# One turn for the slice tokens' half-column products, and a switch time in the planner's model

## The chip, the cores and the metric

The kernel runs on one core of a Trainium2 chip. Its time is the device time of one execution in microseconds; the runs of one kernel are summed up by their median. A core has a matrix engine (PE, whose weight loads are listed as PEld), a vector engine (DVE), a scalar engine (ACT), a small general engine (POOL), and a queue that issues DMAs (SP).

## The reference

For each of 32 batches of x (512 tokens, 256 features, fp32), a graph network and a slice attention are added to x:

```python
# x = x + gnn(layernorm(x), adj);  x = x + ffn(layernorm(x))
out = relu(xn @ mlp1_w + mlp1_b)                 # 512 x 512
h   = out @ W_fc;  att = softmax(leaky_relu(f1[:, None] + f2[None, :]))
out = elu(elu(att @ h)) + out                    # residual
out = relu(out @ mlp2_w + mlp2_b)                # 512 x 256
h   = out @ W_hand; att = softmax(where(adj > 0, leaky_relu(...), -9e15))
x1  = x + relu(elu(elu(att @ h)) + out)
# ffn, 8 heads of 64, 64 slices
w   = softmax((xn2 @ W_x + b_x) @ W_slice / temp)        # per head
tok = (w.T @ (xn2 @ W_fx + b_fx)) / (w.sum(tokens) + 1e-5)
tok = softmax(tok W_q (tok W_k).T / 8) @ (tok W_v)
x   = x1 + (w @ tok) @ W_out + b_out
```

## The kernel before

One batch is one "age". The program is written batch by batch in 22 named steps: `load, norm1, mlp1, h, factors, p, pv, o1` in `front`, `mlp2, h2, e, p2, pv2` in `middle`, `norm2, w, sums, s1T, tokens, att, vo, gg, out` in `back`. No instruction is issued while it is written. A `Recorder` takes each one down with a cost from a model (`_cost`), finds which earlier ones it depends on, and `order` then works out one order for all of them, which `emit` issues. So every instruction has the same line, L255, in the profile, and groups are told apart by their tiles.

The order is made by list scheduling. Each engine takes, of the instructions that can start, the one with the smallest key. A first pass gives each instruction the key age x `PERIOD` + `TURNS[step]` (spread over the step by cost) and plans the first batches; the start times of batch 8 in that plan become the keys of every batch in the second pass, with `HEAD` and `TAIL` added for the first and last three. Instructions of up to four batches are mixed, so that PE finds work of one batch while another waits for DVE, ACT or a DMA. The PSUM tile `mm` has five buffers.

The names in the profile, in the order in which one batch meets them on PE:

- `mm<-xnT,w` (mlp1), `mm<-wfc,o0T` (h), `tr<-ident,ex` (factors), then `mm<-h,pT` (pv): 32 products in four quarters. Of each quarter DVE and ACT make u (`u<-mm,rd`, `m<-u`, two exponentials of m on ACT, `u<-m,u`) and DVE transposes blocks into `u_stage`. When all four are there, SP sends four scatters `scr<-u_stage` to DRAM and one load `o1T<-scr` back, which makes a full transpose; DVE adds o0T (`o1T<-o1T,o0T`).
- `mm<-o1T,w` (mlp2), `mm<-wh,o2T` (h2), then on DVE and ACT the masked logits e, which go through DRAM in the same way (`e_stage`, `p2T`), and `mm<-h,p2T` (pv2).
- x1 and the second layer norm (DVE's xn, `xn_stage`, a load into `xn_raw`), `mm<-weff,xn2T` (w), the softmax of w on DVE, `mm<-xn,w` (sums), and s1 through DRAM (`s_stage`, `s1T`).
- tokens: `mm<-s1T,wfx` are 16 products of 64 columns, each into one half of the partitions of a PSUM tile, and `mm<-nrow,bfx` two more into the halves. These 18 are the half-column products. Then `tok` (DVE), `mm<-tok,wqk`, `qbd`, `sm<-tok,qbd`, `mm<-wvo,tokbd`, `tr<-ident,attbd`, `attT`, `mm<-vo,attT`.
- `mm<-gg,wT` (out): 16 products, two DVE adds into x1 (`x<-mm,x`) and the store.

An fp32 product shows as two rows (two passes) on PE. In the first and the last batch the transposes are made on PE instead of through DRAM.

SP issues DMAs in its order and waits at each for what it needs. Seven loads a batch come back from DRAM scratch, and one buffer of scratch staging (`stage4`, `stage`) is shared by several of them.

Of the kernel before, what the change touches and what calls it, by code (L numbers as in the profile page):

```python
# [13 lines left out]
ENGINES = ("tensor", "vector", "scalar", "gpsimd", "sync")  # L14

TURNS = {
# [4 lines left out]
}  # L21
PERIOD, SPARE = 88.0, 0.00

HEAD, TAIL = (-3.1, -0.9, -0.1), (-1.0, -1.3, -1.0)


SAMPLE, SETUP = 8, 15.0
# [3 lines left out]
P = 128  # L31
# [4 lines left out]
class Recorder:  # L36
# [3 lines left out]
    SIGNAL = 0.06  # L40
    DRAIN = 0.17
    ISSUE, BEGIN, LAND, BEHIND = 0.45, 1.2, 0.9, 2.7
    KEPT = 1
    AHEAD = 3

    def __init__(self, nc):
        self.nc, self.ops, self.logs, self.age, self.step = nc, [], {}, -1, ""
        for engine in ENGINES:
            setattr(self, engine, _Recording(self, engine))

# [23 lines left out]
    def take(self, engine, method, args, kwargs):  # L74
        outs, ins = list(args[:1]), [x for x in args[1:] if isinstance(x, bass.AP)]
        for key, x in kwargs.items():
            if isinstance(x, bass.AP):
                (outs if key in ("out", "accum_out") else ins).append(x)
        op = _Op(engine, method, args, kwargs, self.age, self.step, len(self.ops))
        op.cost, op.lag = self._cost(op, outs[0], ins)  # L80
        before = {}
        for aps, writes in ((ins, False), (outs, True)):
            for ap in aps:
                if not hasattr(ap.tensor, "tag"):
                    continue
                lo, hi, bits = self._region(ap)
                log = self.logs.setdefault(ap.tensor.name, _Log(ap, self.age))
                if log not in op.logs:
                    op.logs.append(log)
                kept = []  # L90
                for entry in log.entries:
                    other, olo, ohi, obits, owrites = entry
                    if other is op:
                        kept.append(entry)
                        continue
                    if (writes or owrites) and olo < hi and lo < ohi and obits & bits:
                        before[other.index] = other
                    if not (writes and lo <= olo and ohi <= hi and not obits & ~bits):
                        kept.append(entry)
                kept.append((op, lo, hi, bits, writes))  # L100
                log.entries = kept
        for other in before.values():
            other.after.append(op)
        self.ops.append(op)

    def _cost(self, op, out, ins):


        def words(ap):
            return ap.size() // ap.ap[0][1]  # L110

        n = words(out)
        if op.method == "dma_start":
            side = next(ap for ap in (out, *ins) if ap.space != bass.MemoryType.DRAM)
            op.moving = out.size() * 4 / (215e3 if side.ap[0][1] <= P // 4 else 320e3)
            return self.ISSUE, 0.0
        if op.engine == "tensor":
            one = max(n / 1200 + 0.002, 0.109)
            if out.ap[0][1] == P // 2:
                one = max(n / 2400, 0.03)  # L120
            return (one if op.method == "transpose" else 2 * one), self.DRAIN
        if op.engine == "scalar":
            pointers = sum(isinstance(op.kwargs.get(k), bass.AP) for k in ("bias", "scale"))
            return 0.06 + n / 1200 + 0.09 * pointers + 0.19 * ("accum_out" in op.kwargs), 0.12
        if op.engine == "vector":
            n = max([n] + [words(x) for x in ins])
            single = op.method in ("tensor_copy", "tensor_scalar")
            fast = single and all(x.space != bass.MemoryType.PSUM for x in ins)
            pointers = sum(words(x) == 1 for x in ins) if n > 1 else 0
            return 0.07 + n / (1920 if fast else 960) + 0.065 * pointers, 0.1  # L130
        if n < 16:
            return (0.1 if op.method == "memset" else 0.3 if op.method == "tensor_scalar" else 1.1), 0.1
        return 0.2 + n / (480 if op.method == "tensor_tensor" else 960), 0.1

    def _schedule(self, ops, key, spare):
# [31 lines left out]
                    t = max(t, min(slots[log.tag]))  # L167
            return t

        done, moved = [], 0.0  # L170
        while len(done) < len(ops):
            best = None
            for e in ENGINES:
                can = [
                    (s, op)
                    for op in waiting[e]
                    if op.age <= oldest + self.AHEAD and (s := start_of(op)) is not None
                ]
                if not can:
                    continue  # L180
                t = max(free[e], min(s for s, _ in can))
                one = min((key(op), op.index, op) for s, op in can if s <= t)
                best = min(best or (t, *one), (t, *one))
            if best is None:
                raise RuntimeError("no operation can start")
            t, _, _, op = best
            waiting[op.engine].remove(op)
            for log in op.logs:
                if log not in until:
                    slots[log.tag].remove(min(slots[log.tag]))  # L190
                    turn[log.queue].pop(0)
                    until[log] = 0.0
            op.start, op.end = t, t + op.cost + op.lag
            free[op.engine] = t + op.cost
            if op.moving:
                moved = max(moved, t + self.BEGIN) + op.moving
                op.end = moved + self.LAND
                free[op.engine] = max(t + op.cost, moved - self.BEHIND)
            for log in op.logs:
                users[log] -= 1  # L200
                until[log] = max(until[log], op.end)
                if not users[log]:
                    slots[log.tag].append(until[log] + self.SIGNAL + spare)
            for later in op.after:
                if later not in left:
                    continue
                if later.engine != op.engine:
                    at = op.end + self.SIGNAL + spare
                else:
                    at = t + op.cost if op.engine == "tensor" else op.end  # L210
                later.ready = max(later.ready, at)
                left[later] -= 1
                if not left[later]:
                    waiting[later.engine].append(later)
            ages[op.age] -= 1
            while not ages.get(oldest, 1):
                oldest += 1
            done.append(op)
        return done

    def order(self):


        steps, keys, ends = {}, {}, {}
# [3 lines left out]
        for (age, step), ops in steps.items():  # L228
            at = TURNS.get(step, -1e5)
            till = TURNS[names[min(names.index(step) + 1, len(names) - 1)]] if age >= 0 else at  # L230
            costs = [op.cost if op.engine == "tensor" else 0.02 for op in ops]
            part = 0.0
            for op, cost in zip(ops, costs):
                keys[op] = age * PERIOD + at + part / sum(costs) * (till - at)
                part += cost
        for op in steps[-1, "setup"]:
            keys[op] = SETUP
        for op in self._schedule([op for op in self.ops if op.age < SAMPLE + 4], keys.get, SPARE):
            ends[op.age] = max(ends.get(op.age, 0.0), op.end)
        period = (ends[SAMPLE] - ends[SAMPLE - 4]) / 4  # L240
        starts = {step: [op.start for op in steps[SAMPLE, step]] for step in TURNS}
# [50 lines left out]
def adj_ffn_kernel(  # L292
# [39 lines left out]
    nc = Recorder(tc.nc)  # L332
# [11 lines left out]
    def mm_tile(shape):  # L344
        return psum.tile(shape, F32, tag="mm", name="mm", bufs=5)
# [52 lines left out]
    def load_x(b):  # L398
# [7 lines left out]
        out=ident, in_=ident, compare_op=OP.not_equal, fill=1.0, base=0,  # L406
# [157 lines left out]
    for p in range(NP):  # L564
        pv = mm_tile([P, D])
# [250 lines left out]
    def back(b, x1):  # L816
# [17 lines left out]
        w = new("w", [P, NT, INNER])  # L834
# [57 lines left out]
        s1T = med("s1T", (P, KD, INNER))  # L892
# [19 lines left out]

        nc.step = "tokens"

        pm = mm_tile([P, NP, G])
        for p in range(NP):
            for k in range(KD):
# [7 lines left out]
        for s in range(2):  # L925
            nc.tensor.matmul(
                pm[ts(s, C)], bfx[:, ts(s, C)], nrow[:, s], start=False, stop=True
            )

        def diagonal(dst, src):  # L930
            nc.vector.tensor_copy(dst(0), src(0))
# [128 lines left out]
```

## Time and profile before

| | us |
|---|---|
| runs (5): median, lowest to highest | 2727.99, 2725.32 to 2731.58 |
| the profiled execution's own time | 2726.07 |
| its span in the profile | 2724.3 |
| PE busy | 2669.1 (98%) |
| DVE busy | 2057.1 (76%) |
| ACT busy | 1118.5 (41%) |
| PE busy from 300 to 2536 us, a stretch of 2236 | 2221.82 |
| PE busy from 2536 us to the end, 188.3 | 167.15 |

A busy PE in these tables is one that has a product in its pipeline; it does not say that the products follow each other at full rate. So the text reads start times in the timeline, where the distance from one row's start to the next, divided by the passes in it, gives the pace. The columns of a timeline row are: start, length, engine, line, operation, out<-in, rows x columns of the array, output size, passes, and in brackets the engine's idle time before it with what ended it.

### The profile page before, as it was taken

Reading aid. Unit: us, or ns where it says so; the run is one execution under the profiler, and the core shown is the slowest. Engines: PE = TensorE matmul, PEld = TensorE weight load, DVE = VectorE, ACT = ScalarE, POOL = GpSimd, SP = SyncE. Lnnn points to the kernel's source line nnn. Section 1 sums busy time; section 2 is a strip of 40 time slices with the busy share of each in tenths; the row PEclk is TensorE's granted clock in tenths of the full one; section 3 lists DMA queues with packets and bytes.
Section 4 is the critical chain, followed back from the end, with each engine's and each line's share of the span. In section 5 each row is a group of like instructions: output and inputs, shape, how many; then the busy total and the mean of one; then the engine's idle time right before and its main releaser. Section 6 shows DMA issues by size and latency. Waiting matters only on the chain.

```text
span 2724.3 us, 34426 instructions
## 1 busy us (share of the span) xinstructions
PE 2669.1 (98%) x11965; PEld 1990.5 (73%) x11965; DVE 2057.1 (76%) x5126; ACT 1118.5 (41%) x2102; POOL 124.8 (5%) x233
## 2 busy tenths in 40 slices
PE   7999999999999999999999999999999999999997
PEld 5777777777777777777777777777777777777765
DVE  6577777887778877778877778777788777788775
ACT  2443344443444433444434444334444334444332
POOL 1000000000000000000000000000000000000000
PEclk9999999999999999999999999999999999999998
DMA  5226455655455555555455556555555555564521
GB/s 167 50 60 167 131 142 145 159 145 148 134 159 139 146 156 139 142 148 159 132 155 139 147 139 155 154 138 140 148 155 136 154 139 144 145 160 128 144 73 47
DMA packets 465077, 375.35 MB, mean 138 GB/s; under 512 B 86532, under 2 KB 382088, under 8 KB 464904
## 3 DMA queue, kind: packets, MB, share of 16 engines
q1 hardware_dynamic: 461568, 371.01, 51.3%
q10 hardware_dynamic: 3336, 2.14, 0.3%
q8 instruction: 95, 1.56, 0.2%
q14 instruction: 78, 0.64, 0.1%
HBM read 197.96 MB, written 175.11 MB: 137 GB/s over the span
## 4 chain that ended last, share of the span: by engine, by line
PE 75%; DMA 11%; DVE 8%; issue 2%; SPq 2%; ACT 2%; POOL 0%; ACTq 0%; DVEq 0%; POOLq 0%
PE mm L255 72%; DMA o1T<-scr 3%; DMA scr<-s_stage 3%; PE tr L255 2%; SPq L255 2%; DMA s1T<-scr 2%; DMA w_raw<-scr 2%; DVE u L255 1%; DVE u_stage L255 1%; PE sm L255 1%; DVE xn_stage L255 1%; DVE xn L255 1%; ACT m L255 1%; DVE w L255 1%; DVE vo L255 0%
## 5 line engine op out<-in xcount | busy, mean ns | idle before, releaser
L255 PE MATMUL mm<-wfc,o0T 128*128 128x257 f32 x2048 | 486.1, 379 | 0.0
L255 PEld LDWEIGHTS mm<-wfc,o0T 128*128 128x128 f32 x2048 | 386.2, 189 | 131.1 <-issue 84.9
L255 PE MATMUL mm<-h,pT 128*128 128x257 f32 (+1 forms) x2048 | 466.9, 382 | 0.4
L255 PEld LDWEIGHTS mm<-h,pT 128*128 128x128 f32 x2048 | 380.0, 189 | 62.5 <-ACT u L255 4.8
L255 DVE TENSOR_TENSOR x<-mm,x 128x512 f32<-128x512 f32 x64 | 44.2, 691 | 294.5 <-PE mm L255 294.5
L255 PE MATMUL mm<-xnT,w 128*128 128x512 f32 x512 | 250.3, 604 | 2.6 <-ACT xnT L255 2.2
L255 PE MATMUL mm<-weff,xn2T 128*128 128x512 f32 x512 | 251.3, 594 | 0.0
L255 PE MATMUL mm<-xn,w 128*128 128x257 f32 x1024 | 243.2, 380 | 6.3 <-DVE w L255 5.5
L255 PE MATMUL mm<-h,p2T 128*128 128x257 f32 x1024 | 242.0, 380 | 0.7 <-ACT p2T L255 0.7
L255 ACT COPY h<-mm 128x257 f32<-128x257 f32 (+1 forms) x384 | 142.6, 371 | 240.7 <-PE mm L255 235.9
L255 PE MATMUL mm<-gg,wT 128*128 128x256 f32 x1024 | 236.0, 379 | 0.0
L255 PE MATMUL mm<-o1T,w 128*128 128x512 f32 x512 | 227.7, 597 | 6.2 <-DVE o1T L255 5.7
L255 PEld LDWEIGHTS mm<-xn,w 128*128 128x128 f32 x1024 | 190.4, 189 | 37.6 <-ACT w L255 5.7
L255 PEld LDWEIGHTS mm<-gg,wT 128*128 128x128 f32 x1024 | 190.1, 190 | 35.0 <-issue 6.5
L255 PEld LDWEIGHTS mm<-h,p2T 128*128 128x128 f32 x1024 | 187.0, 190 | 28.2 <-ACT p2T L255 0.9
L255 PEld LDWEIGHTS mm<-o1T,w 128*128 128x128 f32 x512 | 95.0, 190 | 121.9 <-issue 91.3
L255 DVE STREAM_TRANSPOSE o_stage<-o2T 128x512 f32<-128x512 f32 x64 | 45.6, 712 | 172.1 <-ACT o2T L255 172.1
L255 ACT ACTIVATE e<-e,nmax 128x512 f32<-128x512 f32 x128 | 92.5, 722 | 199.5 <-DVE nmax L255 199.4
L255 ACT ACTIVATE m<-m 128x512 f32<-128x512 f32 x192 | 120.3, 626 | 131.2 <-DVE m L255 131.1
L255 PEld LDWEIGHTS mm<-xnT,w 128*128 128x128 f32 x512 | 93.2, 192 | 69.7 <-issue 51.5
L255 ACT ACTIVATE m<-m,neg 128x512 f32<-128x512 f32 x192 | 138.0, 719 | 3.6
L255 DVE SCALAR_TENSOR_TENSOR u<-m,u 128x512 f32<-128x512 f32 x192 | 131.6, 686 | 9.4 <-ACT m L255 7.8
(144 smaller groups left out, 3923.8 us busy)
## 6 DMA issues: line engine op xcount, KB each, us to landing
scr<-xn_stage SPq DMA_DIRECT2D x240, 128.0 KB, 2.6
scr<-u_stage SPq DMA_DIRECT2D x120, 256.0 KB, 4.1
o1T<-scr SPq DMA_DIRECT2D x30, 1024.0 KB, 5.8
scr<-e_stage SPq DMA_DIRECT2D x120, 256.0 KB, 4.6
p2T<-scr SPq DMA_DIRECT2D x30, 1024.0 KB, 5.3
scr<-w_stage SPq DMA_DIRECT2D x120, 256.0 KB, 4.4
w_raw<-scr SPq DMA_DIRECT2D x30, 1024.0 KB, 6.5
xt<-in_x_dram SPq DMA_DIRECT2D x32, 512.0 KB, 4.6
```

Source lines behind the costliest of these rows:

```text
L255: getattr(getattr(self.nc, op.engine), op.method)(*op.args, **op.kwargs)
```

## The change

Three things are changed. While the 18 half-column products are recorded, `joint` is set, and in the first pass they all get the same key, that of the step's start, so that the planner takes them one after the other. The model gets a time `SWITCH` of 0.14 that it adds wherever PE goes from a half-column product to a whole one or back, and its cost of a half-column pass goes up from at least 0.03 to at least 0.038. And the step times `TURNS`, `PERIOD`, `HEAD` and `TAIL` are others, and the first pass plans one batch more. No instruction is added or removed; only their order on the engines differs.

```diff
 TURNS = {
-    "load": -182.4, "norm1": -141.0, "mlp1": -121.9, "h": -81.6, "factors": -79.1, "p": -73.9,
-    "pv": -53.9, "o1": -53.9, "mlp2": -11.7, "h2": -4.8, "e": 4.9, "p2": 4.9, "pv2": 6.7,
-    "norm2": 28.2, "w": 93.5, "sums": 96.0, "s1T": 101.5, "tokens": 121.9, "att": 133.4,
-    "vo": 142.3, "gg": 151.6, "out": 181.5,
+    "load": 210.7, "norm1": 212.1, "mlp1": 213.6, "h": 289.8, "factors": 309.8, "p": 312.5,
+    "pv": 326.7, "o1": 327.2, "mlp2": 377.6, "h2": 386.3, "e": 387.3, "p2": 391.7,
+    "pv2": 406.4, "norm2": 422.6, "w": 489.3, "sums": 508.3, "s1T": 519.5, "tokens": 539.2,
+    "att": 569.4, "vo": 569.4, "gg": 595.3, "out": 606.3,
 }
-PERIOD, SPARE = 88.0, 0.00
-HEAD, TAIL = (-3.1, -0.9, -0.1), (-1.0, -1.3, -1.0)
+PERIOD, SPARE = 100.3, 0.00
+HEAD, TAIL = (-8.6, 2.8, 1.6), (-4.4, 7.3, 23.6)
...
+    SWITCH = 0.14
...
+        op.joint = self.joint
+        op.half = engine == "tensor" and outs[0].ap[0][1] == P // 2
...
-            if out.ap[0][1] == P // 2:
-                one = max(n / 2400, 0.03)
+            if op.half:
+                one = max(n / 2400, 0.038)
...
+            if op.engine == "tensor" and op.half != half:
+                t, half = t + self.SWITCH, op.half
             op.start, op.end = t, t + op.cost + op.lag
...
+            costs = [0.0 if op.joint else cost for op, cost in zip(ops, costs)]
...
-        for op in self._schedule([op for op in self.ops if op.age < SAMPLE + 4], keys.get, SPARE):
+        for op in self._schedule([op for op in self.ops if op.age < SAMPLE + 5], keys.get, SPARE):
...
         nc.step = "tokens"
+        nc.joint = True
         pm = mm_tile([P, NP, G])
...
+        nc.joint = False
```

In the order that comes out, PE goes to half-column products 35 times instead of 88 in the 32 batches.

More of the change, by code (lines that the diff above doesn't have):

```diff
@@ L47, in __init__ @@
         self.nc, self.ops, self.logs, self.age, self.step = nc, [], {}, -1, ""
+        self.joint = False
         for engine in ENGINES:
@@ L168, in start_of @@
             return t
-        done, moved = [], 0.0
+        done, moved, half = [], 0.0, False
         while len(done) < len(ops):
```

## The prediction

> **What bounds the kernel now.** I read the page's engine rows first, then PE's waits, then one middle period in PE's and SP's timelines.
>
> ```profile
> PE 2669.1 (98%) x11965; PEld 1990.5 (73%) x11965; DVE 2057.1 (76%) x5126; ACT 1118.5 (41%) x2102; POOL 124.8 (5%) x233
> PE mm L255 <- DMA s1T<-scr: 15.2, 15, 8.5
> PE mm L255 <- DVE o1T L255: 5.7, 10, 1.2
> ```
>
> PE bounds it, with few idle gaps; the two PE waits that come back are those for s1T and for o1T. "Busy" hides pace, so here are start times:
>
> ```profile
> 1590.04 9.25 PE L255 MATMUL mm<-h,pT 128*128 128x257 f32 x42
> 1599.47 0.30 PE L255 MATMUL mm<-s1T,wfx 128*64 128x64 f32 x2 [0.18 <-DMA s1T<-scr]
> 1599.70 3.60 PE L255 MATMUL mm<-h,pT 128*128 128x256 f32 x14
> 1603.24 0.69 PE L255 MATMUL mm<-s1T,wfx 128*64 128x64 f32 x16
> 1603.85 2.00 PE L255 MATMUL mm<-h,pT 128*128 128x256 f32 x8
> 1605.78 0.68 PE L255 MATMUL mm<-s1T,wfx 128*64 128x64 f32 x14
> 1606.39 0.65 PE L255 MATMUL mm<-nrow,bfx 4*64 4x256 f32 x4
> 1606.96 1.12 PE L255 MATMUL mm<-xnT,w 128*128 128x512 f32 x2
> ...
> 1619.20 5.77 PE L255 MATMUL mm<-gg,wT 128*128 128x256 f32 x26
> 1625.18 7.13 PE L255 MATMUL mm<-o1T,w 128*128 128x512 f32 x16 [0.21 <-DVE o1T L255]
> 1632.15 3.65 PE L255 MATMUL mm<-wh,o2T 128*128 128x258 f32 x16
> ...
> 1673.11 3.19 PE L255 MATMUL mm<-h,pT 128*128 128x257 f32 x14
> ```
>
> One period is 83.07: 35.14 from the first h,pT to o1T,w (half A), 47.93 from there to the next h,pT (half B). Over 27 periods the timeline gives 35.05 and 47.89. The half-column products come in three visits. Half A has a second chain, through DRAM:
>
> ```profile
> 1611.04 3.37 SPq L255 DMA_DIRECT2D scr<-u_stage  x4
> ...
> 1618.42 0.38 SPq L255 DMA_DIRECT2D o1T<-scr  x1
> ...
> 1624.44 2.50 DVE L255 TENSOR_TENSOR o1T<-o1T,o0T 128x512 f32<-128x512 f32 x4 [0.90 <-DMA o1T<-scr]
> ```
>
> The last u_stage ends at 1611.0, 20.9 after half A began; 7.4 later SP issues the load; it lands 6.0 later; the add takes 0.7; PE starts at once. In nearly all 27 periods o1T,w starts within 0.1 of that add: this chain, not PE, sets half A.
>
> **Part 1, one visit.** Three visits take 0.23 + 0.61 + 1.18 = 2.02 (row starts above). A single one is in the trace, in batch 2:
>
> ```profile
> 277.50 0.60 PE L255 MATMUL mm<-h,pT 128*128 128x256 f32 x2
> 278.02 1.15 PE L255 MATMUL mm<-s1T,wfx 128*64 128x64 f32 x32
> 279.11 0.65 PE L255 MATMUL mm<-nrow,bfx 4*64 4x256 f32 x4
> 279.68 0.70 PE L255 MATMUL mm<-xnT,w 128*128 128x512 f32 x1
> ```
>
> That is 1.66. Two h,pT passes before it take 0.52 where two at the pace of wh,o2T (16 passes in 3.49, the next row starts at 1635.64) take 0.43: 0.09 per entry. Saved per period: 0.36 + 2 x 0.09 = 0.54 of PE time. [...]
>
> The visit now stands behind the last h,pT, about 4.7 later than the first token product stood (11 h,pT products of 0.43). s1T landed 9.45 after the start of half A on average, and is now needed at 13.8: that wait (0.18 here, 0.33 on average) goes. Late next is xnT, landing at 15.3 (median) and needed at about 15.6.
>
> **Part 2, the retimed order.** All of this is read from the new order, its costs from rows. Before o1T,w PE loses 13 gg products (5.6) and two vo (0.86), and gains 12 wfc (5.2) and one transpose (0.1): half A has 1.17 less PE work, half B 1.17 more. PE alone would thus need 35.14 - 0.21 - 0.18 - 0.54 - 1.17 = 33.0 for half A, and 49.1 for half B.
>
> The u chain decides. DVE's queue before had, between tok and the last u_stage, the third quarter's u and u_stage, two xn, u and qbd (1607.08 to 1611.0). Now the third quarter stands before tok, and the fourth's u and u_stage right behind it. DVE's work from its fourth pT operation (ends 2.0 to 2.5 into half A) to tok was 12.9, with 1.9 idle; it becomes 12.9 + 1.85, so tok starts at 16.8. m of the last quarter ends at 16.0; ACT's exponentials (0.63, 0.72 and hops) give 17.5; u 0.6 and u_stage 0.7 make 18.8, against 20.9. With the same 7.4 + 6.0 + 0.7 (SP's order u, xn, o1T is unchanged, and the four xn_stage end at 21.9, before the u scatters are all issued at 22.2) o1T is there at 32.9, as PE arrives at 33.0. Bounds: no gain of the chain (35.05), and PE alone with the small waits in pv gone too (32.5).
>
> So half A goes from 35.05 to 33.0 and half B from 47.89 to 49.06: 82.1 against 82.94, 0.85 less, times 27 = **-23** (bounds +32 and -38).
>
> What else moves: x1's two adds go into the dense DVE stretch of e and w (+1.24, two bn_stats of 0.33 go out of it), while PE needs the last w 0.3 later there; before, w had 0.42 of slack, I keep about 0.15, price 0 to 0.5 a period. Behind these adds on SP now stand the store, the load of xt and p2T's load: the adds end 32.2 after o1T,w, so p2T issues at about 33.1 (33.5 before) and PE needs it at 41 instead of 40. xt lands at about 37.6, and DVE's bn_stats reach it at 38.0; a wait there would hold DVE, and with it f2m, ex and the pT chain queued behind on DVE, but PE needs ex 1.4 after it can be there. The store and gg are 20 later in a period, which nothing in the next batches waits for. tok, tokbd and qbd get longer cover (4 xnT products instead of 1), all at nothing.
>
> **Head.** In batch 2 PE's work from o1T,w to p2T is 27.0 in the new order, 34.1 in the old one. The rows give the chain's length there: o1T,w at 217.16, h,p2T at 256.15, 39.0, waits in between:
>
> ```profile
> 217.16 7.11 PE L255 MATMUL mm<-o1T,w 128*128 128x512 f32 x16
> ...
> 248.84 1.97 PE L255 MATMUL mm<-xn,w 128*128 128x257 f32 x8 [2.28 <-DVE w L255]
> 256.15 2.33 PE L255 MATMUL mm<-h,p2T 128*128 128x257 f32 x10
> ```
>
> DVE's order of e and w there is the same, so the chain stays and 7.1 more of it shows; 2 more where the factors' transposes stand 2.1 instead of 3.7 before h,pT: **+9** (3 to 13).
>
> **Tail.** The wait of 8.5 for s1T (longest of its row) gets 3 more of PE work ahead of it, and p2T's delay too; the last factors get less cover (about 6), e about 3, att about 3. Losses from the last three batches: 32 before, about 29 after: **-3** (-10 to +6).
>
> **Sum.** 2726.07 (span 2724.3) - 23 + 9 - 3 = 2709; the median of the runs lies 1.9 above the profiled one, so **2711**.
>
> **Rivals.** A (slower): u_stage doesn't come earlier, since DVE or ACT is late before tok. Then half A stays 35.05, while half B has its 1.17 more: 27 x 1.17 + 6 = +38, about 2765. It decides from a chain gain below 1.4 a period (1.17 + 6/27). For it: DVE is busy nearly without a gap from w to tok. Against: 1.9 idle in front of tok, and the order puts u_stage first. B (far faster): the chain comes in under PE, and the waits in pv vanish: 32.5 + 49.0 = 81.5, -38 + 6: 2696. C (no gain): the chain gains about 1.4, through a late nrow (slack 0.5) or w, and pays for itself with the head: 2722 to 2733. That the change doesn't join is excluded for the middle (18 in a row in 30 batches).
>
> **Chances.** Forecast 0.50, B 0.20, C 0.16, A 0.14. A measurement here can tell about 0.2% (5.5). Faster 0.73: forecast, B, and a little of C; same 0.12; slower 0.15: A and the rest of C. Range 2692 to 2732: B's end and C; it leaves out A and a little beyond B.
>
> **What would show it.** Right: one s1T row x32 per batch; no PE wait for s1T in the middle; u scatters 18.8 after the first h,pT, o1T,w at 33, periods near 82.1; a wait of about 12 before p2T in batch 2. Wrong: u scatters still at 20.9 with a longer wait of o1T,w (A); new PE waits for w, nrow, xnT or pT (C); more than 40 us of gain or loss in head and tail.

## The result, and the profile after

The changed kernel takes 2735.6 us (median of 35 runs), the kernel before 2727.5 (59 runs). The ratio is 1.0027, with a 95% interval from 1.0020 to 1.0034: **slower by 8 us**, where 2711 was forecast. The profiled executions have spans of 2736.6 and 2724.3.

PE's waits in the changed kernel, the first two rows (total, times, longest):

```profile
PE mm L262 <- DMA xnT<-scr: 16.2, 21, 1.6
PE mm L262 <- DVE o1T L262: 8.9, 10, 1.5
```

The row for s1T's transfer is gone, as forecast. In its place stands a wait for xnT, which the prediction held to be just in time, and the wait for o1T has grown. PE's timeline of one period shows where they sit:

```profile
1593.37 3.62 PE L262 MATMUL mm<-h,pT 128*128 128x257 f32 x16
...
1596.93 10.55 PE L262 MATMUL mm<-h,pT 128*128 128x257 f32 x48
1607.41 1.15 PE L262 MATMUL mm<-s1T,wfx 128*64 128x64 f32 x32
1608.50 0.65 PE L262 MATMUL mm<-nrow,bfx 4*64 4x256 f32 x4
1609.68 3.67 PE L262 MATMUL mm<-xnT,w 128*128 128x512 f32 x8 [0.54 <-DMA xnT<-scr]
...
1626.42 7.11 PE L262 MATMUL mm<-o1T,w 128*128 128x512 f32 x16
```

The join did what it says: one visit, and pv without a break. But PE then stands until xnT lands, 16.2 after the half's start. Half A is 33.1 in this period and 33.66 in the median of 27 (35.12 before, 33.0 forecast); half B is 49.06 in the median, as forecast.

Why xnT is late is read on DVE and on SP's queue in the same period:

```profile
1589.06 1.37 DVE L262 TENSOR_SCALAR xn<-xt,ln_mv,ln_rstd 128x256 f32<-128x256 f32 x4
...
1590.42 0.42 DVE L262 STREAM_TRANSPOSE s_stage<-s 128x256 f32<-128x256 f32 x1
...
1599.95 1.42 DVE L262 STREAM_TRANSPOSE xn_stage<-xn 128x256 f32<-128x256 f32 x4 [0.87 <-DMA scr<-s_stage]
...
1611.69 0.71 DVE L262 STREAM_TRANSPOSE u_stage<-u 128x512 f32<-128x512 f32 x1
```

```profile
1592.43 0.38 SPq L262 DMA_DIRECT2D w_raw<-scr  x1
1592.86 0.56 SPq L262 DMA_DIRECT2D scr<-s_stage  x1
1599.91 0.38 SPq L262 DMA_DIRECT2D s1T<-scr  x1
...
1606.07 0.38 SPq L262 DMA_DIRECT2D xnT<-scr  x1
```

xn_stage and s1_stage are one buffer (tag `stage4`, one copy). So DVE's first xn_stage transpose waits until the last scatter of s1 has landed, and the whole of DVE's queue waits with it: 23.0 us in 24 times. That scatter is late twice over. It stands behind w_raw's 1 MB load, and lands 6.9 after its issue where the three scatters ahead of the load take 2.6 (medians of the trace). And the last s1_stage transpose, which releases all four scatters and the load, now stands on DVE *behind* the four xn operations of the next layer norm. Before, it stood ahead of them:

```profile
1586.39 0.45 DVE L255 STREAM_TRANSPOSE s_stage<-s 128x256 f32<-128x256 f32 x1
1586.76 1.34 DVE L255 TENSOR_SCALAR xn<-xt,ln_mv,ln_rstd 128x256 f32<-128x256 f32 x4
...
1595.88 0.45 DVE L255 STREAM_TRANSPOSE xn_stage<-xn 128x256 f32<-128x256 f32 x1 [0.98 <-DMA scr<-s_stage]
```

The wait was there before as well. What changed is where it ends: xn_stage starts 5.8 into half A in the period before (half A starts at 1590.04) and 6.6 into it now, and xnT lands later by about as much.

The 12.3 us of longer span divide at the fourth and the thirtieth o1T,w: 6.3 more before the fourth (305.4 against 299.1), 1.5 less in the 26 periods between (2153.9 against 2155.4), 7.4 more behind the thirtieth (277.2 against 269.8). The forecast had 9 more, 23 less, 3 less.

### The profile page after: what moved, and what is told of

It reads as the page before. It is cut to its first block, busy times and chain, and to the rows that moved or that the text cites. A ratio compares the mean times of both kernels' runs of the same rounds, so it can differ in the third digit from the quotient of the medians.

```text
span 2736.6 us, 34437 instructions
## 1 busy us (share of the span) xinstructions
PE 2659.1 (97%) x11965; PEld 1991.2 (73%) x11965; DVE 2063.9 (75%) x5126; ACT 1122.1 (41%) x2102; POOL 121.1 (4%) x233
## 5 line engine op out<-in xcount | busy, mean ns | idle before, releaser
L262 PE MATMUL mm<-wfc,o0T 128*128 128x257 f32 x2048 | 508.3, 380 | 0.0
L262 PE MATMUL mm<-h,pT 128*128 128x256 f32 (+1 forms) x2048 | 458.2, 380 | 2.4 <-DVE pT L262 2.2
L262 PEld LDWEIGHTS mm<-wfc,o0T 128*128 128x128 f32 x2048 | 379.0, 190 | 103.3 <-issue 51.9
L262 PE MATMUL mm<-xnT,w 128*128 128x512 f32 x512 | 250.8, 614 | 18.3 <-DMA xnT<-scr 16.2
L262 DVE SCALAR_TENSOR_TENSOR e<-f2b,h,mbias 128x512 f32<-128x512 f32 x128 | 92.7, 745 | 127.1 <-ACT f2b L262 125.9
L262 ACT ACTIVATE w<-w 128x512 f32<-128x512 f32 x128 | 80.7, 631 | 210.0 <-DVE w L262 209.9
```

Source lines behind the costliest of these rows:

```text
L262: getattr(getattr(self.nc, op.engine), op.method)(*op.args, **op.kwargs)
```

## The experiments

Each is a copy of one of the two kernels in which single operations of the finished order are moved, or one buffer or the three shifts of `TAIL` are changed; where an order is changed, the diff gives the move in words. "4th to 30th" is the time from the fourth to the thirtieth o1T,w in the profiled execution, "tail" what follows; half A is a median over 27 periods. Compare by the ratio, since each group of runs has its own median of before (2728 to 2731).

| kernel | us | ratio to before (95%) | half A | 4th to 30th | tail |
|---|---|---|---|---|---|
| before | 2727.5 | 1 | 35.12 | 2155.4 | 269.8 |
| after | 2735.6 | 1.0027 (1.0020 to 1.0034) | 33.66 | 2153.9 | 277.2 |
| split_in_new_order | 2738.8 | 1.0031 (1.0019 to 1.0042) | 33.76 | 2153.1 | 278.2 |
| o1_load_first | 2736.0 | 1.0023 (1.0011 to 1.0035) | 33.28 | 2152.9 | 278.8 |
| s1_flip_first | 2715.0 | 0.9940 (0.9928 to 0.9953) | 32.44 | 2126.0 | 279.6 |
| own_buffer_new_order | 2724.4 | 0.9980 (0.9970 to 0.9990) | 32.88 | 2134.4 | 279.0 |
| flip_and_split | 2736.0 | 1.0019 (1.0008 to 1.0030) | 33.58 | 2151.5 | 276.2 |
| flip_and_spread | 2714.4 | 0.9951 (0.9937 to 0.9966) | 32.42 | 2125.1 | 278.3 |
| flip_and_old_tail | 2703.0 | 0.9903 (0.9889 to 0.9917) | 32.50 | 2126.1 | 267.6 |
| join_in_old_order | 2720.6 | 0.9963 (0.9950 to 0.9975) | 34.89 | 2149.7 | 269.1 |
| old_own_buffer | 2730.1 | 0.9994 (0.9984 to 1.0004) | 35.30 | 2161.2 | 271.2 |
| old_join_own_buffer | 2722.9 | 0.9969 (0.9958 to 0.9980) | 34.80 | 2148.9 | 269.5 |
| old_freed_unjoined | 2730.2 | 1.0009 (1.0001 to 1.0018) | 35.18 | 2159.5 | 267.4 |
| old_join_three_freed | 2693.9 | 0.9871 (0.9857 to 0.9885) | 33.78 | 2125.1 | 267.3 |

**The join alone, in the old order.**

```diff
+ mm = batch b's token products on PE, in order
+ move mm[0..15] (s1T,wfx) directly ahead of mm[16] (first nrow,bfx)
```

> The kernel before with nothing changed but this: each batch's s1T products stand right ahead of its first nrow product, so the visits become one; DVE, ACT, POOL and SP keep their orders. Theory (the join is good, the retiming gives its gain away): the wait for s1T (0.33) and 0.54 of visits leave PE's half A, so nrow ends at about 15.8 after the half's start; xnT lands at 15.3 as before. DVE has 0.6 idle between its last xn_stage and tok that can go, so the fourth u_stage ends at about 20.4 instead of 20.9 and half A takes about 34.5 instead of 35.05; half B stays 47.9. 27 x 0.5 = 13 less than before: about 2714 (2708 to 2720), and head and tail like before's. Rival (the join is worth nothing in any order, since the u chain or xnT is there no earlier): half A stays 35.05 with a longer wait for o1T, 2727. Second rival (one long run of half-width products is slower than in visits): above 2727.

Measured 0.9963, 9 to 10 us less: the join is good by itself, and the third case (a long run is slower) is out. But half A fell only to 34.89, since the fourth u_stage ends at 20.7 and not at 20.4.

**The split put back, in the new order.**

```diff
+ for batches 3 to 27: mm[0] behind pv's 24th product, mm[1..8] behind the 28th
```

> The kernel after with the visits split again in batches 3 to 27: one s1T product behind the 24th h,pT product, eight behind the 28th, seven and nrow behind the 32nd, so that none waits for s1T. Theory (join good, retiming bad): the visits in pv cost 0.8 plus some 0.1 per entry and leaving, pv ends 1.0 to 1.3 later, the fourth u_stage too; nrow ends 0.55 later, where xnT has landed, so xnT's wait (0.93) shrinks to about 0.4. The chain sets half A: about 34.5 instead of 33.7. 25 x 0.7 = +18: about 2753 (2748 to 2760). Rival (in the new order the join gave nothing, because it only waits for xnT earlier): half A stays at 33.7, 2736.

Measured 1.0031, the same as after within the intervals. The rival holds: PE's wait for xnT fell from 16.2 us to 3.1, and pv ended 1.3 later, but u_stage only 0.2 later. In the new order the join saved PE time that PE then spent waiting for xnT.

**One transpose moved.**

```diff
+ for batches 3 to 27: the last s1_stage transpose of batch b directly ahead of
+   the first xn operation of batch b + 3 on DVE
```

> The kernel after with one DVE instruction moved, in batches 3 to 27: the last s1_stage transpose stands ahead of the four xn operations of ln1 instead of behind them, 1.4 earlier. Both theories: s1's last scatter lands 1.4 earlier, xn_stage starts without its wait of 0.87, xnT lands at 15.3 instead of 16.2 and PE's wait for xnT (16.2 us in 21 times) goes. Theory A (two chains of nearly the same length end half A: PE through xnT at 33.2, u_stage to o1T at 33.7): only the periods gain in which o1T stood ready, 6 us in all by the table of periods; the wait for o1T grows from 0.35 to about 1.0 a period: about 2730. Theory B (the late xnT alone took the gain away): 25 x 0.9 = 23 less, about 2713.

Measured 0.9940, 24 below after by the table's ratios. My theory A gave 2730 and is wrong; B has the right time, but not the whole reason. DVE's timeline of one period of this kernel (half A starts at 1582.54):

```profile
1578.35 0.45 DVE L262 STREAM_TRANSPOSE s_stage<-s 128x256 f32<-128x256 f32 x1
1578.72 1.34 DVE L262 TENSOR_SCALAR xn<-xt,ln_mv,ln_rstd 128x256 f32<-128x256 f32 x4
...
1588.25 1.42 DVE L262 STREAM_TRANSPOSE xn_stage<-xn 128x256 f32<-128x256 f32 x4
```

The wait is gone, and not only xnT comes earlier (15.1 instead of 16.2): everything behind xn_stage on DVE does, the fourth u_stage too (18.2 instead of 19.0). Theory A had taken the two chains for independent. They share this one stall. Half A is now 32.44 in the median (32.24 in eight periods in which PE waits neither for xnT nor for o1T: xnT's first product at 15.71 and 16.53 from there to o1T,w), and the 26 periods take 29 us less than before's.

**o1T's load ahead of xn2's scatters.**

```diff
+ for batches 3 to 29: SP's load of o1T directly ahead of the scatters of xn2_stage
```

> The kernel after with one step moved in SP's queue, in batches 3 to 29: the load of o1T stands ahead of the four scatters of xn2_stage instead of behind them. Theory A (SP's queue is part of the chain: the load waits for xn2's scatters to be issued, and these share the DMA engines with u's): the load goes out 0.3 to 1.0 earlier than 7.33 after the u scatters, o1T is there at about 33.1 instead of 33.7, and PE, held by xnT, arrives at 33.2: 27 x 0.4 = 10 less, about 2725 (2720 to 2732); the xnT wait stays, the o1T wait nearly goes. xn2_raw lands about 3 later, at some 37 after the half's start, PE needs xn2T at 44. Theory B (the late xnT alone took the gain away): 2735, no change. A loss would show that xn2 or something behind it on SP is on the path.

Measured 1.0023, no change against after. The load went out 0.4 sooner behind the u scatters, and half A's median fell a little. PE's wait for o1T fell from 8.9 to 2.5 us, but that for xnT was 20.6 instead of 16.2: a shorter u chain alone doesn't pay while xnT is late.

**The stall taken away by a buffer.**

```diff
- stage = new(what + "_stage", [P, D // Q, P], tag="stage4")
+ stage = new(what + "_stage", [P, D // Q, P], tag="raw4" if what == "xn" else "stage4")
```

> The kernel after with every engine's order unchanged; only xn_stage gets the buffer of xn2_raw instead of the one that it shares with s1_stage. Theory (one stall of DVE, 0.87 in front of xn_stage, where it waits for the landing of s1's last scatter, made both ends of half A late: xnT, and through DVE's queue the fourth u_stage; the flip run took it away by an order, this run by a buffer): the stall goes, s1's scatter still lands late, u_stage at about 18.2 and xnT at about 15.3 (its scatters stand behind s1T's load on SP, until 6.6 after the half's start); half A 32.6, about 2716 (2711 to 2721). Rival (the gain of the flip run came from s1's earlier scatter and s1T, not from the stall): 2735.

(The planner is told the old tag, so that no engine's order changes; the lines for that are not shown.) Measured 0.9980: 19.5 us of the flip's 28 between the fourth and the thirtieth o1T,w. The stall did go, but half A is 32.88, not 32.6. The missing part shows in DVE's waits, first after's two rows, then this kernel's:

```profile
DVE xn_stage L262 <- DMA scr<-s_stage: 23.0, 24, 2.1
DVE u L262 <- ACT m L262: 17.8, 37, 1.8
```

```profile
DVE u L262 <- ACT m L262: 28.8, 56, 1.8
```

and on ACT, in the same kernel:

```profile
1594.34 2.18 ACT L262 COPY wT<-w_raw 128x512 f32<-128x512 f32 x4 [1.55 <-DMA w_raw<-scr]
1596.43 0.62 ACT L262 ACTIVATE m<-m 128x512 f32<-128x512 f32 x1
```

Four copies wait for w_raw, and an exponential that DVE needs is queued behind them. The late transpose holds back w_raw's load too, so there is a second stall of DVE, 0.47 a period, that the first had hidden. The flip brings the load forward and so removes both. In the new order this second part is read from the waits; no run there has the own buffer with the copies taken apart.

**Flip and split.**

```diff
+ the moves of s1_flip_first and of split_in_new_order together
```

> The flip run (2715.0) with the visits split in three again in batches 3 to 27, as in split_in_new_order. Theory (the join saves PE time, but where DVE's stall set half A it couldn't show): with the stall gone PE sets half A at 32.4, so now the split's 0.54 of PE and the later end of pv (14.8 instead of 13.5, u_stage 0.5 to 0.9 later) show: half A 33.0 to 33.6, 25 x 0.6 to 1.1 = 15 to 28 more: about 2735. Rival (the join is worth the same 3 in either state): 2718.

Measured 1.0019, 22 us above the flip run by the ratios, where the same split cost 1 to 3 with the stall in place. Half A is 1.1 longer. The theory holds.

**Flip and spread.**

```diff
+ the move of s1_flip_first, and for batches 3 to 27 the four wT copies on ACT: one behind
+   each of the next three u operations of pv or pv2, the fourth behind the first o0T
```

> The flip run with ACT's wT copies taken apart in the same way (three behind the u operations, the fourth behind the first o0T). In the flip run DVE's wait for that exponential is 17.4 us in 37 times, and PE sets half A at 32.4 in most periods already. Theory (PE is the limit there): at most the periods in which o1T still is late gain, 0 to 6 us: 0.992 to 0.994. Rival (the o1T chain is the limit in the flip run too): 0.6 a period, 0.988.

Measured 0.9951, the same as the flip run within the intervals: once the flip is made, PE is the limit in most periods.

**Flip and the old shifts of the tail.**

```diff
-HEAD, TAIL = (-8.6, 2.8, 1.6), (-4.4, 7.3, 23.6)
+HEAD, TAIL = (-8.6, 2.8, 1.6), (-1.0, -1.3, -1.0)
```

> The flip run (0.994 of before) with the three shifts of TAIL put back to before's (-1.0, -1.3, -1.0); TURNS, HEAD and the joined visit stay as in after. Theory 1 (the tail's loss comes from the new shifts, 7.3 and 23.6, with which the last two batches' work is held back): from the 30th o1T,w to the end 270 to 272 instead of 277 to 280, 8 less: 0.991. Theory 2 (it comes from the retimed steps themselves: there is no next batch whose products cover the factors, e and the attention of the last batches): 277 to 282, 0.994 or more.

Measured 0.9903, and a tail of 267.6 instead of 279.6: theory 1, by 12 us instead of 8. PE's timeline, first three of the tail's gaps in after, then two in this kernel:

```profile
2586.06 0.29 PE L262 MATMUL sm<-ident,fm 128*128 128x128 f32 x1 [2.00 <-DVE fm L262]
...
2659.13 0.66 PE L262 MATMUL tr<-ident,e 128*128 128x128 f32 x4 [2.79 <-ACT e L262]
...
2675.85 0.70 PE L262 MATMUL mm<-tok,wqk 128*128 128x256 f32 x2 [2.08 <-DVE tok L262]
```

```profile
2623.28 5.39 PE L262 MATMUL mm<-xn,w 128*128 128x257 f32 x16 [2.44 <-DVE w L262]
...
2641.19 1.98 PE L262 MATMUL mm<-s1T,wfx 128*64 128x64 f32 x32 [5.46 <-DMA s1T<-scr]
```

The waits for fm, e and tok of over 2 us are no longer there; a wait for s1T is back, 5.5 instead of before's 8.5.

**The old order, freed.** Four more runs in the order of before: the own buffer without the join and with it, and both stalls taken away, with the join and without.

> The kernel before with the own buffer for xn_stage alone: no join, no retiming. Theory of the two close limits: PE with its three visits reaches o1T at 34.8 to 34.9 whatever DVE does, so only the wait for o1T (0.1 to 0.2 a period) goes: 3 to 6 less than before, about 2723. Rival (the stall alone sets half A in the old order as well): half A 34.1, 27 x 0.95 = 25 less, about 2702.

> join_in_old_order with the own buffer for xn_stage, orders unchanged. Theory (in the old order too two limits lie close together: PE, which the join shortens, and DVE's chain with its stall of 0.98, which the buffer shortens; either alone gives some 0.2 a period, both together about 1): u_stage at about 19.8, xnT at 14.7, PE through nrow (15.8) and 18.0 of work at o1T at 33.9; half A about 34.0 instead of 34.85: 27 x 0.85 = 23 less than 2720.6: about 2698 (2693 to 2706), the fastest so far, with the old head and tail. Rival (u_stage is set by DVE's work between pT and tok, not by the stall): 2718 to 2721.

Measured 0.9994 and 0.9969: the buffer changed nothing that the intervals show, with the join or without. DVE's waits say why. First before, then old_own_buffer:

```profile
DVE xn_stage L255 <- DMA scr<-s_stage: 19.6, 22, 1.6
```

```profile
DVE u L255 <- ACT m L255: 31.4, 35, 1.8
```

(before, the wait of u for m was 7.8 us). The stall moved to the exponential behind ACT's copies. For that reason the second expectation was too good by some 24 us (by the ratios). The first was by 3, which its interval can't tell, but the wait for o1T, which was to go, grew from 5.7 us to 8.7. So the copies were taken apart as well:

```diff
+ old_join_own_buffer, with the wT copies placed as in flip_and_spread
```

> old_join_own_buffer with ACT's four wT copies taken apart: one behind each of the next three u operations of pv, the fourth behind the first o0T, instead of four in a row in front of an exponential. What old_join_own_buffer showed: with the stall at xn_stage (0.94 a period) gone, DVE waits 1.16 for that exponential instead, which stands on ACT behind the copies, and these wait for the landing of w_raw. Theory (in the old order half A hangs on w_raw's landing twice, through DVE's buffer and through ACT's copies; the join shows its whole worth only when both are off): DVE reaches tok and u_stage about 1.0 earlier (u_stage 19.6), PE through nrow (15.8) and 18.0 of work sets half A at 33.9 instead of 34.8: 27 x 0.9 = 24 less: 0.988 of before, about 2703 where before has 2730. Rival (u_stage is set by something else still, POOL or PE): no change, 0.997.

Measured 0.9871, **35 us less than before: the fastest of all**, with the old `TURNS`, `HEAD` and `TAIL`. u_stage ends at 19.65 and half A is 33.78, near the 19.6 and 33.9 expected.

> old_join_three_freed without the join: the kernel before with the own buffer for xn_stage and the wT copies taken apart, its three visits as they were. It closes the square of join and freed chain in the old order. Theory (two limits of nearly the same length: PE with the three visits, and DVE's chain): PE alone still comes to o1T at 34.8 (nrow ends at 16.8, then 18.0 of work), the o1T wait nearly goes, half A 34.8 instead of 33.9 with the join and 35.05 before: 27 x 0.9 = 25 more than 2694, ratio 0.996 to before; the join is then worth 25 with the chain freed, against 9 in the old order as it was. Rival (freeing the chain did it all and the join adds nothing): 0.987.

Measured 1.0009: both freed, but without the join, nothing is gained. I had expected 0.996, since I reckoned PE at o1T at 34.8 and DVE ahead of it; but u_stage stayed at 21.0, for DVE's next wait is for PE:

```profile
DVE rd L255 <- PE mm L255: 40.0, 64, 2.5
```

(13.7 before). The quarters of pv come later with the visits between them, and DVE's chain starts from each quarter. So the join shortens both limits, PE's and, through pv, DVE's.

## Why the prediction was wrong, and where it was right

**Part 1 holds in its PE work.** One visit in place of three, the wait for s1T gone from the middle, and "1.66" for the visit is what the trace shows: in the flip run, where no wait follows, s1T starts at 1596.59, nrow at 1597.68 and xnT's product at 1598.25. The 32 passes take 1.09 there, as in batch 2 of before (278.02 to 279.11) and in the changed kernel (1607.41 to 1608.50). In the changed kernel's visit the 32 weight loads start in pairs, 6 to 7 ns apart within a pair, a pair every 55 to 59 ns.

**The step that failed is "Late next is xnT, landing at 15.3 (median) and needed at about 15.6".** That 15.3 was a landing of the old order, carried over, and it had no room: over 26 periods of the old trace the median is 15.5, from 14.7 to 17.2, and the flip run needs xnT at 15.7. The new order has the last s1_stage transpose behind the four xn, and xnT lands at 16.2. Worth 28 us in the 26 periods: with this one transpose back ahead of xn, they gain 29 on before, more than the 23 forecast, and half A is 32.44, next to rival B's 32.5. The own buffer shows that 19.5 of the 28 come from the stall at xn_stage itself.

About 5 us of the changed kernel's 26 periods went at a lower granted clock. In three periods of the middle half A is 35.9, 35.3 and 35.7. There PE waits 1.1, 1.3 and 1.6 for xnT, and at some time between 0.4 us before the end of the wait and 0.7 behind it the granted clock goes to 0.5 for 3.4 us. In the first of them eight passes take 5.20 to the next row's start, where 3.5 would do at the pace of o1T,w (16 in 6.94); the 5 is an estimate from that for all three:

```profile
1195.43 5.37 PE L262 MATMUL mm<-xnT,w 128*128 128x512 f32 x8 [1.11 <-DMA xnT<-scr]
1200.63 0.59 PE L262 MATMUL mm<-tok,wqk 128*128 128x256 f32 x2
```

Waits of 1.4, 1.3 and 1.1 in three other periods brought no such stretch, so no rule can be read from them. In the kernel before the granted clock is 1.00 from 50.6 to 2658.3 us, with waits of PE of up to 2.3 in this stretch.

**The u chain: the time of tok came out by luck.** "DVE's work from its fourth pT operation to tok was 12.9, with 1.9 idle; it becomes 12.9 + 1.85": the 1.85 was put into the idle time, and the idle time at nothing. But some 0.9 of it was the wait at xn_stage, in front of the added work, and the work behind it did not fill it. The medians of after (25 periods): the fourth pT operation ends at 1.26 (not 2.0 to 2.5), the work takes 14.6 (14.75 forecast), and 0.88 is idle. A start reckoned too late and a stall put at nothing cancel, and tok starts at 16.8 as reckoned; in the flip run, without the stall, it starts at 15.9. u_stage ended at 19.0 instead of 18.8, as u still waited 0.37 for ACT behind tok. Together with xnT on PE's side, the later of the two made half A 33.66 in the median, a gain of 1.46 (1.34 in the mean without the last of the 27 periods, in which the shifts of `TAIL` make half A 39.5), where half B costs 1.14. So the gain came out around rival A's point of 1.4 "a period", though u_stage did come earlier, and A's mechanism was not the one. Rival C had nearly the size (a chain gain that just pays), with w or nrow as its cause where the runs show xnT; among the signs of being wrong the prediction does name a PE wait for xnT.

One stalled instruction moved all that DVE does behind it: with the stall of 0.88 gone, tok starts 0.90 earlier and the last u_stage 0.85 (medians).

**Half B and the head held.** Half B was forecast at 49.06 and is 49.06; p2T lands 40.6 after o1T,w and is used at 41.2 (41 forecast). The head cost 6.3 of a forecast 9 (3 to 13). Its chain kept its length, as forecast: from the third o1T,w (224.24) to h,p2T (263.83) 39.6, before 39.0. The forecast wait of about 12 is there in two parts: PE waits 9.1 in all (7.38 in the row below, 1.34 and 0.41 behind it), and with a granted clock of 0.52 the 14 passes take 5.87 to the next row's start instead of 3.0.

```profile
251.61 6.04 PE L262 MATMUL mm<-xn,w 128*128 128x257 f32 x14 [7.38 <-ACT w L262]
257.48 0.27 PE L262 MATMUL sm<-ident,fm 128*128 128x128 f32 x1
```

**The tail's "-3" failed, by its shifts.** I read the covers off the new order (factors about 6, e about 3, attention about 3, against the 8.5 of s1T). By the brackets of PE's rows, the last batch's factors wait 5.7 (2.00, 1.44 and 2.22), near the forecast; its e waits 4.6 (2.79, 1.30 and 0.46), and tok to attT of the batch before it 4.1 (2.08, 0.43, 0.76 and 0.78). PE is also slower for some time behind the first two: 12 passes of h,pT take 4.65 instead of 2.6, at a granted clock of 0.57, and 32 of h,p2T 9.16 instead of 6.9, at 0.77. These losses come from `TAIL`, whose shifts of 7.3 and 23.6 the prediction never costed as an edit of its own: with the old ones the same `TURNS` have a tail of 267.6 against before's 269.8, 2.2 less and near the -3 that was forecast, and s1T's wait there is 3.0 shorter, as it said.

**What the retiming is worth.** With the stalls gone, old and new `TURNS` take the same 2125 to 2126 us from the fourth to the thirtieth o1T,w. The retiming gains nothing there that the join in the old order does not, and costs 6 to 10 in the head and, with its shifts, 7 to 12 in the tail.

What stays open: the head was not tried by itself, and no run shows which of `HEAD` and `TURNS` makes its 6 us.

## What to carry to other kernels

When an order changes, redo every landing time from the new order, and follow each transfer back to the instruction that releases its *buffer*: here one transpose, 1.4 later, cost 24 us, most of it through a staging buffer that two steps share. Before idle time of an engine is used as room for moved work, ask what ends it and whether the moved work stands in front of that wait or behind. And where limits lie close together, try repairs in pairs: in the old order the join alone gave 0.4%, freeing DVE's chain alone nothing, both together 1.3%.

## What the runs showed of the hardware

In the changed kernel a scatter of 128 KB issued 0.43 behind a load of 1 MB on the same queue landed after 6.93 (median of 18), its three predecessors after 2.62.
